# A planned two-layer graph network: attention products of two head groups together, bias reliefs in a way of their own, and some transposes on TensorE

## The chip, the cores and the metric

The kernel runs on one core of one Trainium2 chip. The metric is the device time of one execution in microseconds (us). The time before is the median of three runs, 3202.94 us (3202.18 to 3202.97). All computation is in float32.

## The reference

There are 64 graphs with 256 nodes of 256 features, and an adjacency matrix of zeros and ones for each. Two layers follow each other.

```python
# layer 0
h = _gat(x, adj, W1, a1, Fout)          # Wh = h @ W; e = leaky_relu(Wh @ a[:F] + (Wh @ a[F:]).T)
h = _gat(h, adj, W2, a2, W2.shape[1])   # softmax over axis 1 of where(adj > 0, e, NEG), then @ Wh
h = _layernorm(residual + h, g_ln1, b_ln1)
ff = jnp.matmul(jax.nn.relu(jnp.matmul(h, w_ff1) + b_ff1), w_ff2) + b_ff2
x = _layernorm(h + ff, g_ln2, b_ln2)
# layer 1: q, k, v of 8 heads with 32 features each
scores = jnp.einsum('bhid,bhjd->bhij', q, k) / np.sqrt(dh)
attn = jax.nn.softmax(scores, axis=-1)
for r in range(4):                      # adj holds 0 and 1 only, so two of the four count
    mask = (adj_matrix == r)[:, None]
    out = out + jnp.einsum('bhij,bhjd->bhid', attn * mask, v_r)
x = _ln(src + out @ Wo + bo, g1, beta1)
x = _ln(x + jax.nn.gelu(x @ W1 + b1, approximate=False) @ W2 + b2, g2, beta2)
```

The feed-forward width is 1024.

## The kernel before, in words

The unit of work is a pair of graphs: 32 pairs, each with 512 nodes. `whole_way` (L687) takes one pair from its input to its output: `gat_layers` (L363), `feed_forward` with relu, `attention` (L524), `feed_forward` with gelu (L472), and the store of the result. These functions are generators. Every `yield` ends a step of TensorE work and says which events the next step waits for, the name of a stage that one pair at a time may hold ("gat", "attention" or "ff"), and how many of the eight PSUM banks it takes.

`run` (L208) is a planner that runs while the program is built. It keeps a clock for each engine (`START` sets where they begin) and up to three pairs in progress. At each turn it picks the piece of work that can begin first. On TensorE a step that isn't feed-forward goes ahead of a feed-forward step, so feed-forward fills the gaps of the others. Work for VectorE, ScalarE, GpSimd and the DMA queue of SyncE (SP) is handed in with `put` (L153): an assumed duration, events that it waits for, a rank, and buffers that it needs or frees. `keep_order` (L197) fixes the order found as the order on each engine. Assumed durations thus set the order only; on the chip the engines wait for each other by semaphores.

Stages and lines that matter here:

- **Start.** Constants and weights are loaded on the SP queue in the order in which they are written (L648 to L662). Pair 0's inputs come first, through `load` (L264); for other pairs `load` is put to the plan when the pair before them starts. The loads are xT (input with features on partitions, one buffer), adjT (four buffers) and x (five buffers).
- **Graph layers.** L383 multiplies the input by the weights, `addends` (L288) turns node scores into rows on all partitions, on TensorE for pair 0 (L316) and through DRAM for all others (`row`, `rows`), `gat_weights` (L341) makes the weights e, and L397 and L408 apply them. The stage "gat" is held to the end of the second layer.
- **Layernorm and transposing.** `layernorm` (L421) works on VectorE with a power on GpSimd. `transposed` (L447) turns 32x32 blocks on VectorE (L454), stores them to DRAM (L459, `home`) and gathers them in four DMAs (L465) into yT, the operand with features on partitions. This is done for both graphs of the pair, b = 0 and 1, and at three stages: before the first feed-forward (stage 0 in the change's numbering), before attention (1) and before the second feed-forward (2).
- **Feed-forward.** L483 is 128x512 with eight steps of four matmul records, L499 is 128x256 with eight steps of eight; ScalarE evacuates the first (L486), VectorE adds the second to the rows (L419).
- **Attention.** L520 makes queries and keys, L512 values. The heads of a graph come in two groups of four, so a pair has four groups n. `scores` (L543) multiplies queries and keys in four row tiles of 32 (L550) and takes four banks; ScalarE exponentiates (L557), VectorE masks (L561, `m`, seven buffers) and adds the two halves (L565, `h`, four buffers). `products` (L572) multiplies weights and values in four column tiles of 32 (L579, L582), then VectorE takes reciprocals (L591) and divides (L592). `into_rows` (L596) is the output projection (L601).
- **Reliefs.** Biases are moved into the layernorm offsets; what that adds elsewhere is subtracted again by `relieve` (L669, matmuls at L675) and `relieve_values` (L680, L683). They are steps of pair 0's own way, L692 to L703.

A group's order in attention is written by hand (L605 to L636); its core is:

```python
for n in range(4):
    yield [*masked[n], *valued[:2 + n // 2 * 2]], None, 1
    divided.append(products(n))
    if n < 2:
        yield [], None, 1
        valued.append(values(v[1], 1, n, yT))
        yield [], None, HQ
        scores(n + 2)
```

One written float32 matmul appears in the trace as two matmul records, each with a weight load; a transpose as one.

Of the kernel before, what the change touches and what calls it, by code (L numbers as in the profile page):

```python
# [10 lines left out]
F32 = mybir.dt.float32  # L11
# [7 lines left out]
P = 128  # L19
# [7 lines left out]
MS = 7  # L27
START = {"tensor": 12.0, "vector": 11.0, "scalar": 12.0, "gpsimd": 0.0, "sync": 33.0}
# [3 lines left out]
def two_layers(ctx: ExitStack, tc: tile.TileContext, t: dict, out: bass.AP, flag: bass.AP):  # L32
# [91 lines left out]
    def bank():  # L124
# [12 lines left out]
    free = {name: [0.0] * n for name, n in (("bank", 8), ("a", 2 * HQ), ("m", MS), ("h", HQ), ("yb", 2), ("yT", 3), ("yTa", 1),  # L137
                                             ("xT", 1), ("adjT", 4), ("x", 5))}
# [69 lines left out]
    def run(ways, together):  # L208


        going, ways = [], iter(ways)
        while True:
# [8 lines left out]
            for n, (way, events, name, banks) in enumerate(going):  # L221
                if alone.get(name) in (None, way) and all(e.time is not None for e in events):
                    at = begins("tensor", max([e.time for e in events], default=0.0), "bank" if banks else None, banks)
                    if at is not None:
                        times.append((at, n))
# [8 lines left out]
            if engine == "tensor":  # L234
# [3 lines left out]
                takes("bank", g[3])  # L238
                step = next(g[0], None)
                if step is None:  # L240
                    going.remove(g)
# [22 lines left out]
    def load(pair, at=None):  # L264
# [7 lines left out]
        def adjT():  # L272
            to["adjT"] = io.tile([P, 4, N], I32, name="adjT", bufs=4)
            nc.sync.dma_start(to["adjT"], t["adjT"][rows].rearrange("b (c p) n -> p (b c) n", p=P))

        def x():
            to["x"] = io.tile([P, 4, D], F32, name="x", bufs=5)
# [4 lines left out]
        for emit in (xT, adjT, x):  # L282
            takes(emit.__name__)
# [4 lines left out]
    def addends(y, there, at, layer, pair):  # L288
# [6 lines left out]
        ratio, rows, at_home = small.tile([P, 4], F32, name="ratio"), None, {}  # L295
# [14 lines left out]
        if pair == 0:  # L310
            yield [there], None, 4
            rows, copied = work.tile([P, 8, 4, 32], F32, name="rows"), []
# [9 lines left out]
            return rows, ratio, copied  # L322
# [9 lines left out]
        def spread():  # L332
            nc.sync.dma_start(rows.rearrange("p q n c -> p (q n c)"),
                              at_home["row"].rearrange("j q c -> (j q c)").partition_broadcast(P))

        rows = work.tile([P, 8, 4, 32], F32, name="rows")
        there = put("vector", 0.2, turn, there, rank=0)
        there = put("sync", 0.4, store, there, rank=0, lag=1.9)
        return rows, ratio, [put("sync", 0.4, spread, there, rank=0, lag=3.8)]

    def gat_weights(y, at, rows, ratio, there, to, empty, b):  # L341

        e = work.tile([P, 2, N], F32, name="e", bufs=2)
        sums, rs = small.tile([P, 2], F32, name="sums"), small.tile([P, 2], F32, name="rs")

        def weigh(j):
            k = 2 * b + j
# [806 lines left out]
```

## Time and profile before

| What | Value |
|---|---|
| median of three runs | 3202.94 us |
| profiled execution: time, span | 3197.83 us, 3195.9 us |
| mean granted TensorE clock | 0.993 |
| TensorE (PE) busy | 3146.7 us, 98% |
| VectorE (DVE) busy | 2174.8 us, 68% |
| ScalarE (ACT) busy | 1065.0 us, 33% |
| GpSimd (POOL) busy | 193.0 us, 6% |
| L499 matmuls, both feed-forwards | 919.9 us |
| L483 matmuls, both feed-forwards | 896.2 us |
| L579 and L582 (products), in the chain that ended last | 7.5% and 1.7% of the span |

The span runs from the first to the last instruction on the chip; the execution's own time lies 1.9 us above it. The span is not the median: the three timed runs are executions of their own. Busy times of TensorE overlap, because matmuls are pipelined, so the distance from one start to the next says more than the length of one record. The reader should look at which engine the chain that ended last runs on, at the places where that engine stands idle and for whom it waits, and at how the starts follow each other where it does not stand idle.

### The profile page before, as it was taken

The numbers are of one execution on the slowest core, as the hardware profiler recorded it, in microseconds if no ns is written. First come the engines' busy times: TensorE is split into PE (matmuls) and PEld (weight loads), VectorE is DVE, ScalarE is ACT, GpSimd is POOL, SyncE is SP. The second block draws the span as 40 slices with busy tenths as digits, with TensorE's granted clock in tenths as the row PEclk, the third lists the DMA queues.
The fourth block names the chain that finished last, engine by engine and source line by source line (L and its number), as shares of the span: only waits on it lengthen the run. The fifth ranks groups of instructions, "written<-read, shape, count | busy, mean of one in ns | idle before, by whom it ended". The sixth has DMA issues, their size and how long they took to land.

```text
span 3195.9 us, 44346 instructions
## 1 busy us (share of the span) xinstructions
PE 3146.7 (98%) x16494; PEld 1999.0 (63%) x16494; DVE 2174.8 (68%) x5537; ACT 1065.0 (33%) x1994; POOL 193.0 (6%) x262
## 2 busy tenths in 40 slices
PE   5999999999999999999999999999999999999998
PEld 4666755675576567556756765675567567656645
DVE  3776676767766866767577668667675776686655
ACT  2323323333343233333332432333333324323332
POOL 0000000000000000000000000000000000000000
PEclk8999999999999999999999999999999999999999
DMA  6111311221132123112211321231122113112110
GB/s 199 47 50 63 113 37 57 82 90 34 34 106 67 37 63 113 40 53 83 89 34 34 106 67 37 69 107 43 51 85 87 34 34 113 60 42 65 61 32 28
DMA packets 217438, 211.52 MB, mean 66 GB/s; under 512 B 23040, under 2 KB 175744, under 8 KB 217216
## 3 DMA queue, kind: packets, MB, share of 16 engines
q1 hardware_dynamic: 217216, 208.62, 20.7%
q8 instruction: 132, 2.16, 0.3%
q14 instruction: 90, 0.74, 0.1%
HBM read 141.18 MB, written 67.36 MB: 65 GB/s over the span
## 4 chain that ended last, share of the span: by engine, by line
PE 98%; DMA 1%; SPq 1%; DVE 0%; issue 0%; POOL 0%; POOLq 0%; DVEq 0%
PE ps L499 28%; PE ps L483 28%; PE ps L579 7%; PE ps L512 7%; PE ps L520 7%; PE ps L550 4%; PE ps L601 4%; PE ps L383 3%; PE ps L397 3%; PE ps L408 3%; PE ps L582 2%; DMA ff<-in_L_gnn_bo 0%; DMA xT<-in_xT 0%; SPq L465 0%; DMA yT<-home 0%; PE ps L675 0%
## 5 line engine op out<-in xcount | busy, mean ns | idle before, releaser
L499 PE MATMUL ps<-w_L_gnn_w_ff,ff 128*128 128x256 f32 x2048 | 462.8, 381 | 0.0
L483 PE MATMUL ps<-yT,w_L_gnn_w_ff1p 128*128 128x512 f32 x1024 | 447.4, 594 | 12.1 <-DMA yT<-home 12.1
L499 PE MATMUL ps<-w_L_gnn_W,ff 128*128 128x256 f32 x2048 | 457.1, 381 | 0.0
L483 PE MATMUL ps<-yT,w_L_gnn_W1p 128*128 128x512 f32 x1024 | 448.8, 594 | 7.9 <-DMA yT<-home 7.9
L499 PEld LDWEIGHTS ps<-w_L_gnn_w_ff,ff 128*128 128x128 f32 x2048 | 385.8, 190 | 74.4 <-issue 24.3
L499 PEld LDWEIGHTS ps<-w_L_gnn_W,ff 128*128 128x128 f32 x2048 | 386.7, 190 | 67.3 <-issue 16.5
L561 DVE TENSOR_TENSOR m<-a,adjT 128x512 f32<-128x512 f32 x512 | 339.4, 683 | 76.3 <-ACT a L557 76.3
L557 ACT ACTIVATE a<-ps 128x512 f32<-128x512 f32 x512 | 264.3, 603 | 330.5 <-issue 242.7
L444 POOL TENSOR_TENSOR rstd<-rstd,mhalf 128x2 f32<-128x2 f32 x256 | 192.3, 751 | 2995.9 <-DVE rstd L433 2990.1
L419 DVE TENSOR_TENSOR x<-ps,x 128x512 f32<-128x512 f32 x256 | 173.3, 677 | 263.6 <-PE ps L499 260.6
L483 PEld LDWEIGHTS ps<-yT,w_L_gnn_w_ff1p 128*128 128x128 f32 x1024 | 194.8, 191 | 243.2 <-issue 230.2
L483 PEld LDWEIGHTS ps<-yT,w_L_gnn_W1p 128*128 128x128 f32 x1024 | 194.9, 191 | 235.9 <-issue 219.5
L486 ACT ACTIVATE ff<-ps,c_L_gnn_b_ff 128x512 f32<-128x512 f32 x256 | 175.5, 686 | 445.1 <-PE ps L483 444.7
L514 DVE TENSOR_TENSOR v<-ps,b_L_gnn_bv 128x512 f32<-128x512 f32 x128 | 84.2, 658 | 320.8 <-PE ps L512 320.8
L486 ACT ACTIVATE ff<-ps,c_L_gnn_b 128x512 f32<-128x512 f32 x256 | 175.3, 685 | 345.2 <-PE ps L483 344.9
L512 PE MATMUL ps<-wv,yTa 128*128 128x512 f32 x512 | 247.3, 605 | 0.0
L358 ACT ACTIVATE xw<-xw,rs 128x258 f32<-128x258 f32 (+1 forms) x256 | 116.2, 501 | 375.5 <-DVE rs L353 375.5
L591 DVE RECIPROCAL s<-ps 128x256 f32<-128x256 f32 x128 | 224.1, 1751 | 10.0 <-PE ps L582 10.0
L565 DVE TENSOR_TENSOR h<-a 128x256 f32<-128x256 f32 x512 | 203.6, 418 | 35.3 <-PE ps L582 34.2
L431 DVE BATCH_NORM_STATS2 st<-x 128x6 f32<-128x256 f32 x512 | 207.8, 406 | 2.3
L374 ACT ACTIVATE xw<-ps 128x260 f32<-128x260 f32 (+1 forms) x256 | 97.5, 385 | 326.7 <-PE ps L383 287.3
L348 DVE SCALAR_TENSOR_TENSOR e<-rows,ratio 128x256 f32<-128x256 f32 x256 | 121.9, 476 | 70.7 <-DMA rows<-row 62.7
(96 smaller groups left out, 3412.1 us busy)
## 6 DMA issues: line engine op xcount, KB each, us to landing
home<-yb SPq DMA_DIRECT2D x192, 256.0 KB, 2.1
yT<-home SPq DMA_DIRECT2D x768, 64.0 KB, 2.0
rows<-row SPq DMA_DIRECT2D x62, 512.0 KB, 4.2
xT<-in_xT SPq DMA_DIRECT2D x32, 512.0 KB, 4.5
adjT<-in_adjT SPq DMA_DIRECT2D x32, 512.0 KB, 5.8
x<-in_x SPq DMA_DIRECT2D x32, 512.0 KB, 6.8
out<-x SPq DMA_DIRECT2D x32, 512.0 KB, 3.2
w_L_gnn_w_ff1p<-in_L_gnn_w_ff1p SPq DMA_DIRECT2D x1, 1024.0 KB, 7.9
```

The source lines that it names most:

```text
L431: nc.vector.bn_stats(st[:, j, :], rows[j])
L444: power = put("gpsimd", 0.8, lambda: nc.gpsimd.tensor_tensor(rstd, rstd, mhalf[:, :2], ALU.pow), there)
L483: nc.tensor.matmul(p1, lhsT=w1[:, c, m * P:(m + 1) * P], rhs=yT[c], start=c == 0, stop=c == KC - 1)
L486: there = put("scalar", 0.6, lambda m=m, p1=p1: nc.scalar.activation(f[m], p1, func, bias=b1[:, m:m + 1]), took(1.72), relieved, function= ...
L499: nc.tensor.matmul(p2[:, j * D:(j + 1) * D], lhsT=f[m][:, (2 * j + b) * P:(2 * j + b + 1) * P], rhs=w2[:, m, :], start=m == 0, stop=m == N ...
L512: nc.tensor.matmul(ps, lhsT=yT[:, b, c, jc * P:(jc + 1) * P], rhs=wv[:, c].rearrange("p r m -> p (r m)"), start=c == 0, stop=c == KC - 1)
L520: nc.tensor.matmul(ps, lhsT=w[:, d, c * P:(c + 1) * P], rhs=yT[:, :, d, :], start=d == 0, stop=d == KC - 1)
L557: nc.scalar.activation(a[n][o], ps[o], AF.Exp)
L561: nc.vector.tensor_tensor(m[n][o], a[n][o], adj, ALU.mult)
L565: nc.vector.tensor_tensor(h[n][o], a[n][o][:, :N], a[n][o][:, N:], ALU.add)
L579: nc.tensor.matmul(po[o * DH:(o + 1) * DH, :N], lhsT=v[b][:, jc, at:at + DH], rhs=e[o][:, jc * N:(jc + 1) * N], start=r == jc == 0, stop=r ...
L591: there = put("vector", 1.68, lambda: nc.vector.reciprocal(s, po[:, N:]), there, rank=0)
```

## The change

Five things are changed.

1. In attention, `products` of both head groups of a graph are issued in one step, without another step between them. It waits for the masks of both groups. The two value steps of the second graph follow, then scores 2 and 3, then the products of groups 2 and 3, and then both output projections. The buffers of m and h become eight each.
2. The reliefs leave pair 0's way and become a way of their own, `reliefs`, which runs beside the three pairs until it is done.
3. `hurried` names five stages: stage 0 of pairs 0 and 1, stage 2 of pair 30, stages 1 and 2 of pair 31. There `transposed_on_tensor` replaces the way through DRAM: 16 matmuls by the identity for each graph, in column tiles of 32, into one bank that ScalarE copies out. `addends` uses TensorE for pair 1 as well.
4. Pair 1's inputs are loaded right after the weights of the first feed-forward, ahead of all other weights. adjT has three buffers and x four.
5. The stage "gat" is given up after the first graph layer, and an event keeps the next pair's first application of weights behind the end of the second layer of the pair before. The tiles e and rows are planned as buffers with a due time. Some assumed times differ.

The diff, cut to its core:

```diff
-MS = 7
-START = {"tensor": 12.0, "vector": 11.0, "scalar": 12.0, "gpsimd": 0.0, "sync": 33.0}
+HURRIED = 2
+START = {"tensor": 12.0, "vector": 11.0, "scalar": 12.0, "gpsimd": 0.0, "sync": 40.0}
...
-            for n, (way, events, name, banks) in enumerate(going):
+            for n, (way, events, name, banks, *more) in enumerate(going):
                 if alone.get(name) in (None, way) and all(e.time is not None for e in events):
                     at = begins("tensor", max([e.time for e in events], default=0.0), "bank" if banks else None, banks)
+                    for needs in more:
+                        at = None if at is None else begins("tensor", at, needs)
...
                 step = next(g[0], None)
                 if step is None:
+                    together -= g[0] is besides
...
-        if pair == 0:
-            yield [there], None, 4
-            rows, copied = work.tile([P, 8, 4, 32], F32, name="rows"), []
+        if pair < HURRIED:
+            yield [there], None, 4, "rows"
...
+            yield [e[b][1], *([] if b or not pair else [through_gat[pair - 1]])], None, 2
+            if b == 0:
+                z = work.tile([P, 4, D + 4], F32, name="xw", bufs=2)
...
+        done_with("gat")
+        at_home, ratio, there = yield from addends(z, there, D, 1, pair)
...
+    def hurried(pair, stage):
+
+        return (pair, stage) in ((0, 0), (1, 0), (NPAIR - 2, 2), (NPAIR - 1, 1), (NPAIR - 1, 2))
+
+    def transposed(y, ready, to, b, pair, stage):
+
+        if hurried(pair, stage):
+            to[b] = ready
+            return
...
+    def transposed_on_tensor(y, to):
+
+        for b in range(2):
+            if b == 0:
+                yield [to[b]], None, 1, "yT"
+                to["yT"] = work.tile([P, 2, 4, KC * 64], F32, name="yT", bufs=3)
+            else:
+                yield [to[b]], None, 1
+            p = bank()
+            for c in range(KC):
+                for j in range(2):
+                    for q in range(4):
+                        at = q * 64 + c * 32
+                        nc.tensor.matmul(p[32 * q:32 * q + 32, c * N + j * P:c * N + (j + 1) * P],
+                                         lhsT=y[:, 2 * b + j, at:at + 32], rhs=ident, start=True, stop=True)
+
+            def copy(b=b, p=p):
+                nc.scalar.activation(to["yT"][:, b].rearrange("p a (ck i) -> p ck a i", i=32),
+                                     p.rearrange("p (ck a i) -> p ck a i", a=4, i=32), AF.Copy)
+
+            to[b] = put("scalar", 0.55, copy, took(0.75), frees=["bank"])
+
+    def feed_forward(y, normal, w, func, relieved, gb, pair, stage):
         w1, b1, w2 = w
+        onwards = stage == 0
+        if hurried(pair, stage):
+            yield from transposed_on_tensor(y, normal)
...
-            there = took(2.37)
+            there = took(2.2)
...
-        for n in range(4):
-            yield [*masked[n], *valued[:2 + n // 2 * 2]], None, 1
-            divided.append(products(n))
-            if n < 2:
-                yield [], None, 1
-                valued.append(values(v[1], 1, n, yT))
-                frees_at(clock["tensor"], ["yTa"] * n)
-                yield [], None, HQ
-                scores(n + 2)
-            if n == 2:
-                yield divided[:2], None, 1
-                into_rows(0)
+        for n in (0, 2):
+            yield [*masked[n], *masked[n + 1], *valued[:2 + n]], None, 2
+            divided += [products(n), products(n + 1)]
+            if n == 0:
+                for jc in range(2):
+                    yield [], None, 1
+                    valued.append(values(v[1], 1, jc, yT))
+                frees_at(clock["tensor"], ["yTa"])
+                for later in (2, 3):
+                    yield [], None, HQ
+                    scores(later)
         frees_at(masked[3][-1].time, ["adjT"])
-        yield divided, None, 1
-        into_rows(1)
+        for b in range(2):
+            yield divided[2 * b:2 * b + 2], None, 1
+            into_rows(b)
...
-    landed = {name: at_time(us) for name, us in (("ln0", 14.0), ("ff0", 20.0), ("attention", 31.0), ("ff1", 38.0))}
+    landed = {name: at_time(us) for name, us in (("ln0", 14.0), ("ff0", 23.0), ("attention", 38.0), ("ff1", 45.0))}
     loaded = {0: load(0, 11.0)}
     ln = [layernorm_weights("L0_gnn_g_ln1", "L0_gnn_b_ln1", "L0_gnn_b_ff2")]
     ff0 = (weights("L0_gnn_w_ff1p"), column("L0_gnn_b_ff1"), weights("L0_gnn_w_ff2"))
+    loaded[1] = load(1, 26.0)
...
+    def reliefs():
+        yield [landed["ff0"]], None, 1
+        put("vector", 0.0, lambda: None, relieve(ff0[1], ff0[0], ln[0][2]), event=relieved[0])
+        yield [landed["attention"], *differences], None, 3
+        there = [relieve(bq, wq, ln[1][2]), relieve(bk, wk, ln[1][2]), relieve_values(ln[1][2])]
+        put("vector", 0.15, lambda: nc.vector.tensor_scalar(bqs, bq, SCALE, None, ALU.mult), *there, event=relieved[1])
+        yield [landed["ff1"]], None, 1
+        put("vector", 0.0, lambda: None, relieve(ff1[1], ff1[0], ln[2][2]), event=relieved[2])
...
+    run(reliefs(), (whole_way(pair) for pair in range(NPAIR)), 3)
```

## The prediction

> **What bounds the kernel now.** I read the busy times first, then the chain that ended last, then TensorE's own waits, then its timeline.
>
> ```profile
> PE 3146.7 (98%) x16494; PEld 1999.0 (63%) x16494; DVE 2174.8 (68%) x5537; ACT 1065.0 (33%) x1994; POOL 193.0 (6%) x262
> PE 98%; DMA 1%; SPq 1%; DVE 0%; issue 0%; POOL 0%; POOLq 0%; DVEq 0%
> ```
>
> TensorE (PE) is the bound, and the chain is TensorE nearly throughout. VectorE (DVE) comes second, a third idle. Between 200 and 3050 us the list of TensorE's waits is empty. So only three things can shorten this kernel: less TensorE work, fewer lost moments between matmuls that follow each other, or a smaller idle head and tail. The idle is all here:
>
> ```profile
> 21.49 5.61 PE L397 MATMUL ps<-xw,e 128*128 128x258 f32 x16 [4.06 <-ACT xw L358]
> 31.81 5.41 PE L408 MATMUL ps<-xw,e 128*128 128x256 f32 x16 [2.81 <-ACT xw L358]
> 44.10 6.28 PE L383 MATMUL ps<-w,xT 128*128 128x260 f32 x16 [3.42 <-DMA xT<-in_xT]
> 62.49 3.75 PE L483 MATMUL ps<-yT,w_L_gnn_w_ff1p 128*128 128x512 f32 x4 [12.11 <-DMA yT<-home]
> 102.42 0.95 PE L675 MATMUL ps<-c_L_gnn_boc,w_L_gnn_Wqp 128*128 128x1 f32 x8
> ...
> 3097.49 6.99 PE L483 MATMUL ps<-yT,w_L_gnn_W1p 128*128 128x512 f32 x12 [7.87 <-DMA yT<-home]
> ```
>
> Columns are start, length, instructions, and in brackets the idle time before. The two largest waits are for yT, the transposed rows that go through DRAM. The reliefs after 102 us stand in a stretch that is already full. After each idle time the matmuls are slow: 16 of L397 take 5.61 us here, 3.76 later.
>
> The middle, attention of one pair:
>
> ```profile
> 1075.31 1.88 PE L520 MATMUL ps<-yTa,w_L_gnn_Wkp 128*128 128x512 f32 x4
> 1077.03 1.88 PE L512 MATMUL ps<-wv,yTa 128*128 128x512 f32 x4
> 1078.84 1.15 PE L550 MATMUL ps<-qT,kT 32*128 32x256 f32 x16
> 1079.91 1.98 PE L520 MATMUL ps<-yTa,w_L_gnn_Wqp 128*128 128x512 f32 x4
> 1081.73 1.88 PE L520 MATMUL ps<-yTa,w_L_gnn_Wkp 128*128 128x512 f32 x4
> ...
> 1100.56 1.07 PE L579 MATMUL ps<-a,v 128*32 128x256 f32 x16
> 1101.44 1.05 PE L579 MATMUL ps<-m,v 128*32 128x256 f32 x16
> 1102.31 0.61 PE L582 MATMUL ps<-h,ones 128*32 128x256 f32 x8
> 1102.85 1.99 PE L601 MATMUL ps<-w_L_gnn_Wo,oT 128*128 128x256 f32 x8
> ```
>
> Lengths overlap, so read from start to start. L520 before L512 takes 1.72 us; L512 before the scores (L550) takes 1.81; L520 after the scores takes 1.82. Nothing waits there: about 0.1 us is lost at every change of tile shape.
>
> [...] here 4 L483 after 12.11 us of idle take 3.75 us, later 1.88.
>
> **Part 1, products in one stretch.** Single records of the trace give the price of a shape change. A group of four tiled matmuls repeats every 216 ns, 128x512 every 429.
> - Into a tiled stretch: 522 instead of 429, +0.093 us. First matmul after it: 533 instead of 429, +0.104.
> - Scores: second group 320 (+0.104), leaving 324 (+0.108).
> - Products: second group 240 (+0.024), leaving 329 (+0.113).
>
> So products alone lose 0.093+0.024+0.113+0.104 = 0.334 us, scores alone 0.093+0.104+0.108+0.104 = 0.409, and scores directly followed by products 0.093+0.104+0.108+0.024+0.113+0.104 = 0.546. Over all records I count 53 joined stretches, 75 scores alone and 75 products alone: 28.9+30.7+25.1 = 84.7 us. After: 64 double products lose 21.4, and 128 scores alone 52.4. The double ones need masks of the scores just made (four ACT operations of 0.6 and eight DVE operations, 4 x (0.68+0.42) = 4.4 us), so they hardly follow scores at once and the joined stretches go. Sum 73.7: **gain 11.0**. In the new order scores 2 and 3 can touch if eight banks are free; the two products and two values before them hold four, feed-forward one more, so I assume one pair in four: 8 x 0.409 = **3.3** (0 to 13.1).
>
> The price is a longer wait inside attention: about 5.5 us from second scores to products, some 8 after the fourth, 4.5 for two reciprocals (1.75 each) and divisions before the second output projection, together some 18 us instead of 11. Feed-forward of other pairs, 4 x 13.8 = 55 us per pair, covers it; uncovered it is TensorE idle. Behind a waiting product on TensorE queue all other pairs' matmuls. In the trace the last mask or half is ready 0.7 to 3.3 us ahead of its product. The plan prices mask and half at 0.61 and 0.36 (0.68 and 0.42 measured), so eight run 0.5 us late. With steps of 1.72 us I let a quarter of 64 stretches wait 0.25 us: **loss 4** (0 to 25).
>
> **Part 2, head: reliefs in idle time, pair 1 early, transposes for pairs 0 and 1.** Idle before: 7.34+0.52+0.90+4.06+0.81+2.81+3.42+12.11 = 32.0. The first four (12.8) precede other available work and stay. After that the first relief (3.6 us, already in idle time), pair 1's first products (3.8) and later products, and the attention reliefs (4, now in the full part) can fill. Pair 0's rows are normalised at 42 and 44; from there its feed-forward needs two transposes and copies, about 46 instead of 62.5. I leave 3.7 us of new idle: 16.5, so 15.5 gained (10 to 19). Slow-clock excess is 1.85 (L397)+1.79 (L408)+2.61 (L383)+1.87 (L483) = 8.1; the first and about 1.7 stay, 4.5 gained.
>
> Added: each transposed half is 16 multiplications, two records each as at L579, so 8 groups of four. Width is half of L579's: 0.108 us if it scales, 0.216 if a floor holds. I take 0.13 (L316, 128 columns: 1.06/8), the weight load being 0.11: 1.04+0.334 = 1.37 us (1.2 to 2.1). Four halves: 5.5. Pair 1's row transposes: 2 x 1.06 = 2.1. **Head: 15.5+4.5-5.5-2.1 = gain 12.4** (4 to 18).
>
> Queues: on SP pair 1's three loads (0.4 to 0.6 us each) pass all attention weights. The xT issue waits for L383 to have read the old xT (15.4 us); SP stood at 15.5 there, so that wait costs under 1 us, and the 1.5 MB behind it some 5 us at about 350 GB/s. Attention weights come 5 us later, needed at 102 in before: covered. Each hurried stage takes two stores, eight gathers (0.43 each) from SP and two 0.70 turns from DVE, and gives ACT two copies of some 0.6: ACT is 33% busy, nothing. POOL keeps its work. Fewer x and adjT buffers cost nothing, as loads land in 5.8 to 6.8 us and a pair has 97; the early release of the graph stage gives nothing where TensorE is full.
>
> **Part 3, tail.** The idle 7.87 and the slow 1.7 after it go: pair 30's second projection starts at 3080.8, its rows can be ready near 3088, and work lasts until 3089.3. Added six halves, 8.2; next is pair 31's second output, with less filler: 1. **Gain 9.6-8.2-1 = 0.4** (-4 to 4). The last 10 us (normalise, store) stay.
>
> **Sum.** 11.0+3.3-4+12.4+0.4 = 23.1. The profiled execution took 3197.83 (span 3195.9 and 1.9 around it): 3174.7. The median of runs is 5.1 above it, 3202.94: **3180**.
>
> **Rivals.**
> - Larger: scores 2 and 3 touch in every pair (+9.8) and no products wait (+4): 3166. For it: banks empty quickly when feed-forward is in its second half. Against: that half holds a bank. 12%.
> - Head gives nothing, because late weights or transposes of 2.1 us (+7.3 over ten) eat it: 3192 to 3195. For it: the DMA engines are at 0.8 to 0.9 in the first 50 us. Against: pair 1's loads pass the attention weights, and only pair 0's own inputs and the first feed-forward's weights stay ahead. 10%.
> - Within 0.2%: waits of some 0.4 us per stretch cancel all: 3200. 8%.
> - Slower: the double products' wait becomes TensorE's bound. 23.1+4 over 64 stretches: from 0.42 us each the gain is gone, and from 0.53 us it is over 6.4 us (0.2%) slower. At 0.7 us: 3180-4+45 = 3221. For it: each stretch waits for twice the masks, and the plan underprices DVE by a tenth. Against: no wait of any kind on TensorE in 2850 us now. 10%.
> - That products are not adjacent: excluded, both are emitted in one step and the order is fixed.
>
> The forecast has 60%, 3170 to 3190. The range reaches to the larger gain and to the lost head: 3164 to 3196. Faster by over 0.2% (about what a measurement of this kernel can tell from no change): 82%, same 8, slower 10.
>
> **What would show it.** 80 tiled records of L579 and L582 in a row in about 4.5 us, 64 such stretches; no TensorE wait in the middle (right) or an entry at L579 from DVE (wrong); first feed-forward near 46 us; reliefs before 60 us; a tiled 128-column group at 0.13 us; no 7.87 gap at 3089. A loss of more than 0.4 us at each double stretch would make the prediction wrong.

## The result, and the profile after

| | median | range | runs |
|---|---|---|---|
| after | 3214.3 us | 3211.77 to 3217.1 | 6 |
| before, on the same chip | 3202.56 us | 3197.13 to 3203.07 | 6 |

The changed kernel takes 1.0041 of the time before (95% interval 1.0028 to 1.0054). It is slower by 12 us, where 23 us less were predicted. The profiled execution took 3215.46 us with a span of 3213.5 us and a mean granted clock of 0.996.

Busy times and the chain that ended last, from the page of after:

```profile
PE 3157.0 (98%) x16830; PEld 2016.3 (63%) x16830; DVE 2182.1 (68%) x5525; ACT 1085.4 (34%) x2030; POOL 193.9 (6%) x262
...
PE 75%; DVE 15%; DMA 8%; issue 1%; ACT 1%; SPq 0%; POOL 0%; DVEq 0%; POOLq 0%; ACTq 0%
```

TensorE is as busy as before, but the chain has changed: only 75% of it lies on TensorE now, where it was 98%. That does not mean that TensorE stands idle for a quarter of the span: the chain goes over to VectorE and DMA wherever TensorE had to wait at all, and follows them back from there. How long TensorE waits between 200 and 3060 us, and where, its list of waits says (for whom, us in total, times, longest; idle times under 0.15 us are not listed). In the kernel before, this list is empty:

```profile
PE ps L409 <- ACT xw L368: 28.8, 27, 2.8
```

L409 applies the weights of the first graph layer (L397 before). It waits 27 times, about once in each pair. How the 17.6 us between the two spans came about is read from a sum that I call **lost time**: elapsed time less each matmul record at the distance at which its kind repeats without a stop (0.429 us at 512 columns, 0.216 at 256, 0.219 and 0.2175 at 260 and 258, 0.054 in a group of four tiles; transposes, reliefs and the start at nothing). The ideal is 3034.0 us for both kernels. It is cut by the work done, counted in ideal time: the first 200 us, up to 2900, the rest.

| lost time, us | head | middle | tail | after the last matmul |
|---|---|---|---|---|
| before | 63.1 | 74.2 | 15.1 | 9.4 |
| after | 47.8 | 103.9 | 18.4 | 9.2 |
| predicted change | -12.4 | -10.3 | -0.4 | 0 |
| measured change | -15.3 | +29.7 | +3.4 | -0.2 |

The head is better than predicted. The middle is where the prediction fails, by 40 us, so first to what could have been slow there and isn't. The double products, TensorE's timeline of one pair in after (start, length, instructions):

```profile
1083.52 1.07 PE L629 MATMUL ps<-a,v 128*32 128x256 f32 x16
1084.41 1.05 PE L629 MATMUL ps<-m,v 128*32 128x256 f32 x16
1085.27 0.61 PE L632 MATMUL ps<-h,ones 128*32 128x256 f32 x8
1085.70 1.05 PE L629 MATMUL ps<-a,v 128*32 128x256 f32 x16
1086.57 1.05 PE L629 MATMUL ps<-m,v 128*32 128x256 f32 x16
1087.43 0.61 PE L632 MATMUL ps<-h,ones 128*32 128x256 f32 x8
1087.97 3.70 PE L560 MATMUL ps<-wv,yTa 128*128 128x512 f32 x8
```

80 records in 4.45 us from start to start, and no bracket behind any L629: no product waits for its masks.

Now a pair whose L409 waits, from the timeline of all engines in after; the issues of DMAs stand under SPq:

```profile
952.19 13.90 PE L531 MATMUL ps<-yT,w_L_gnn_w_ff1p 128*128 128x512 f32 x32
...
952.97 0.39 SPq L755 DMA_DIRECT2D out<-x  x1
...
954.25 0.24 DVE L333 STREAM_TRANSPOSE blocks<-rise 128x64 f32<-128x64 f32 x1
...
954.52 0.54 SPq L337 DMA_DIRECT2D row<-blocks  x1
...
957.63 0.37 SPq L284 DMA_DIRECT2D x<-in_x  x1
...
959.06 0.34 SPq L341 DMA_DIRECT2D rows<-row  x1
...
964.61 0.48 DVE L358 SCALAR_TENSOR_TENSOR e<-rows,ratio 128x256 f32<-128x256 f32 x1 [5.16 <-DMA rows<-row]
...
967.71 0.91 ACT L368 ACTIVATE xw<-xw,rs 128x258 f32<-128x258 f32 x2 [4.33 <-DVE rs L363]
...
968.27 4.13 PE L409 MATMUL ps<-xw,e 128*128 128x258 f32 x10 [2.18 <-ACT xw L368]
```

And the same piece of a pair in the timeline of before:

```profile
923.49 0.54 SPq L330 DMA_DIRECT2D row<-blocks  x1
...
926.30 0.34 SPq L333 DMA_DIRECT2D rows<-row  x1
...
930.52 0.48 DVE L348 SCALAR_TENSOR_TENSOR e<-rows,ratio 128x256 f32<-128x256 f32 x1 [2.14 <-DMA rows<-row]
...
934.81 3.64 PE L397 MATMUL ps<-xw,e 128*128 128x258 f32 x16
```

Read it as a race. The node scores leave TensorE with L393, are turned on VectorE (L333), stored as a row (L337), spread over all partitions (L341), made into weights (L358) and into scaled rows on ScalarE (L368); then L409 may start. In its place TensorE runs eight steps of feed-forward, 13.7 us, and that number is the planner's: it stands in both kernels. In before the rows are used 4.2 us after their issue (926.30 to 930.52) and TensorE never stops. In after it is 5.55 us (959.06 to 964.61), and 2.18 us are lost. Beside the rows two transfers of 512 KB are at work: the store of a finished pair (out), and the load of the next x, which had to wait for that store, because x has four buffers instead of five. SyncE's own waits in after, 200 to 3090 us:

```profile
SPq L284 <- DMA out<-x: 37.5, 13, 4.4
```

There is no such line in before. Mean over pairs 2 to 31, worked out from the starts in the traces, for all kernels that matter (us; a "gap" of 0.43 from the start of the last record before L409 to L409 is no wait):

| kernel | turn to row store | to spread | to first weight | turn to first weight | first weight to L409 | gap |
|---|---|---|---|---|---|---|
| before | 0.28 | 2.84 | 4.32 | 7.44 | 4.32 | 0.43 |
| after | 0.29 | 3.31 | 5.52 | 9.13 | 3.74 | 1.54 |
| x late | 0.29 | 3.12 | 4.85 | 8.26 | 3.87 | 0.83 |
| weights in one piece | 0.39 | 3.55 | 5.11 | 9.06 | 3.05 | 0.55 |
| "gat" to the end | 0.36 | 3.68 | 4.91 | 8.95 | 4.03 | 0.78 |
| plan told 5.6 us | 0.37 | 2.92 | 6.02 | 9.31 | 5.16 | 0.35 |
| small x load | 0.28 | 3.21 | 4.99 | 8.48 | 3.83 | 0.98 |
| small x load and out store | 0.28 | 2.44 | 4.54 | 7.26 | 4.60 | 0.52 |

The plan itself believes 6.85 us from turn to first weight (0.2 for the turn, 0.15 for handing it on, 0.4 and 1.9 for the store, 0.4 and 3.8 for the spread). Before took 0.6 us more than that, and after takes 2.3 more. The gaps of after add up to 46.2 us over these 30 pairs, those of before to 12.9: 33.3 us are lost there. Another 2.8 us go at the second record of L409, and 3.1 to a lower clock: behind its two longest waits, of 2.18 and 2.79 us, TensorE runs at half the clock for 3.41 us each. One of the two (window; length; busy time of PE, PEld, DVE, ACT, POOL; granted clock; DMA share; GB/s):

```profile
968.90:972.20 3.30, 3.30 (x9) 2.55 (x8) 0.00 (x0) 2.32 (x6) 0.00 (x0) 0.50 0.16 43
```

These make 39 us. The middle loses 29.7 more than before, so some 9 are gained in it elsewhere, most of them by the double products (experiment 2).

Where the path grew can be read from the landing times of the same transfers. From turn to first weight it is 1.69 us longer than in before. The row store lands 0.19 us later (2.92 us after its issue, 2.73 in before), the spread is issued 0.28 later after that landing (0.39, 0.11 in before), and the spread itself lands 1.20 later (5.35, 4.15 in before). So most of it is transfers that take longer, and a smaller part is the spread's wait for its turn on the queue. In the 27 pairs of after in which the load or the store was under way for over 0.5 us beside the spread, it lands after 5.51 us, in the other three after 3.99.

### The profile page after: what moved, and what is told of

Read it like the earlier page. It is cut to its first block, busy times and chain, and to the rows that moved or that the text cites. A ratio compares the mean times of both kernels' runs of the same rounds, so it can differ in the third digit from the quotient of the medians.

```text
span 3213.5 us, 44988 instructions
## 1 busy us (share of the span) xinstructions
PE 3157.0 (98%) x16830; PEld 2016.3 (63%) x16830; DVE 2182.1 (68%) x5525; ACT 1085.4 (34%) x2030; POOL 193.9 (6%) x262
## 4 chain that ended last, share of the span: by engine, by line
PE 75%; DVE 15%; DMA 8%; issue 1%; ACT 1%; SPq 0%; POOL 0%; DVEq 0%; POOLq 0%; ACTq 0%
PE ps L547 24%; PE ps L531 16%; PE ps L568 7%; PE ps L560 7%; PE ps L629 7%; DMA rows<-row 5%; PE ps L600 4%; PE ps L409 4%; PE ps L651 3%; DVE e L360 2%; DVE e L358 2%; DVE st L447 2%; DVE x L435 2%; DMA out<-x 2%; PE ps L632 2%; DVE x L453 2%
## 5 line engine op out<-in xcount | busy, mean ns | idle before, releaser
L611 DVE TENSOR_TENSOR m<-a,adjT 128x512 f32<-128x512 f32 x512 | 350.9, 685 | 112.9 <-ACT a L607 112.9
L368 ACT ACTIVATE xw<-xw,rs 128x258 f32<-128x258 f32 (+1 forms) x256 | 115.9, 500 | 418.9 <-DVE rs L363 418.9
L560 PE MATMUL ps<-wv,yTa 128*128 128x512 f32 x512 | 238.7, 599 | 0.0
L615 DVE TENSOR_TENSOR h<-a 128x256 f32<-128x256 f32 x512 | 214.1, 418 | 0.0
L358 DVE SCALAR_TENSOR_TENSOR e<-rows,ratio 128x256 f32<-128x256 f32 x256 | 122.2, 477 | 126.5 <-DMA rows<-row 116.8
```

Source lines behind the costliest of these rows:

```text
L560: nc.tensor.matmul(ps, lhsT=yT[:, b, c, jc * P:(jc + 1) * P], rhs=wv[:, c].rearrange("p r m -> p (r m)"), start=c == 0, stop=c == KC - 1)
L611: nc.vector.tensor_tensor(m[n][o], a[n][o], adj, ALU.mult)
L615: nc.vector.tensor_tensor(h[n][o], a[n][o][:, :N], a[n][o][:, N:], ALU.add)
```

## The experiments

Each median stands beside that of the kernel before in the same batch; the bracket is the 95% interval of the ratio. Before moves by up to 1.7 us between these batches, so a difference between kernels of two batches holds to a microsecond or two.

**1. One cause at a time.** The fewer buffers alone on the kernel before; the double products with their buffers on it; x's load put behind its own pair's rows; and the plan told the longer landing of the rows.

```diff
 # b_buf, on before
-                                             ("xT", 1), ("adjT", 4), ("x", 5))}
+                                             ("xT", 1), ("adjT", 3), ("x", 4))}
 # b_pp, on before: as b_buf, m and h eight each, and the products' and output projections' order of the change
 # a_xlate, on after: the x load is put to the plan only when the pair's own rows are under way
+        if "load x" in to:
+            put("sync", 0.5, to["load x"], *there, rank=3, lag=4.0, needs="x", event=loads[2])
 # a_rowlag, on after
-        return at_home, ratio, [put("sync", 0.4, spread, there, rank=0, lag=3.8, needs="rows")]
+        return at_home, ratio, [put("sync", 0.4, spread, there, rank=0, lag=5.6, needs="rows")]
```

> The kernel before with one edit: x in four buffers and adjT in three, as in the change. Theory (the load of x now waits for the output store, stands on the SP queue between the row store and the spread of rows, and shares the DMA engines with it, so the graph layer's weights come late and TensorE waits at its first application): this alone makes TensorE wait at L397 in most pairs, 0.5 to 1.5 us each, 3215 to 3240 us. Rival (early release of the graph stage or the merged products cause the waits): no waits at L397, 3203 within 3 us.

> The kernel before with the products of both head groups in one stretch and the buffers that this needs (m and h eight each, x four, adjT three), nothing else of the change. My prediction had a gain of 9 to 11 us from the fewer changes of tile shape. Theory: that gain is there, but the graph layer's first application waits as in the changed kernel, 20 to 35 us, so about 3215 to 3225. Rival (the waits come from the early release of the graph stage): no waits, about 3192.

> The changed kernel, with the load of x planned only once the pair's own rows of the first graph layer are spread, so that it no longer stands between row store and rows. x is needed only at the end of the second graph layer. Theory: most of the 33 us of waits at the first application of the graph weights go, 3182 to 3192. Rival (the rows are late by themselves, or the stage's early release puts the step too early): the waits stay, 3208 to 3216.

> The changed kernel, with one number of the plan altered: the spread of rows is assumed to land 5.6 us after its issue in place of 3.8 (the trace of the changed kernel shows 5.3 to 6.2 from issue to the first use). Nothing on the chip becomes faster; the plan only places the graph step later and other TensorE work before it. Theory: TensorE has other work at that point, so the waits mostly go, 3182 to 3195. Rival (no other TensorE work is there at that time): unchanged at 3214.

Measured, against 3199.41: b_buf 3207.45, 1.0024 [1.0016, 1.0033]; b_pp 3206.02, 1.002 [1.0013, 1.0028]; a_xlate 3190.49, 0.9968 [0.9956, 0.998]; a_rowlag 3177.9, 0.993 [0.9917, 0.9944].

One number of the plan takes the changed kernel from 1.0041 to 0.993 of before, some 35 us. The rows are not used sooner for it: they land after 4.82 us (5.35 in after) but are used after 6.02. What it does is that the planner puts other work in front of the weights and of L409. What is left of the waits from 200 to 3060 us in a_rowlag:

```profile
PE ps L409 <- ACT xw L368: 1.4, 1, 1.4
PE ps L568 <- ACT yTa L583: 0.4, 1, 0.4
```

So enough other work was there: in 28 of the 30 pairs 15.5 or 17.2 us of steps now stand ahead of L409, and the middle loses 66.0 us instead of 103.9. Fewer buffers cost 8 us in before too, though L397 waits only 3.0 us there: its lost time grows in the middle (74.2 to 82.5) and a little in the head (63.1 to 65.1). The rows come later there too (4.93 instead of 4.32 us). The list of waits shows only a part: by the starts of its records, L397 loses 8.6 us in the middle of b_buf (0.3 in before), 4.4 at its first record and the rest at its second and at the first two of the second graph, much of it in stops too short for the list. Both b_buf and b_pp were expected to take 3215 us or more; waits of the size of those in after did not come. The double products on top of it give 9.6 us in the middle (82.5 to 72.9) and lose 11.3 in the tail (14.7 to 26.0), where without transposes TensorE waits 16.5 us for the last pair's attention operand.

**2. Other ways to shorten the race; the parts of the gain.** On after: both weights of a graph as one piece, and "gat" held to the end of the second layer as before. On a_rowlag: products apart as before (r_nopp), no transposes in the last pairs (r_notail).

```diff
 # a_weigh, on after
-        there = put("vector", 0.9, lambda: weigh(0), *there, rank=0, needs="e")
-        there = put("vector", 1.0, lambda: weigh(1), there, rank=0, frees=["rows"] * b)
+        there = put("vector", 1.9, lambda: (weigh(0), weigh(1)), *there, rank=0, needs="e", frees=["rows"] * b)
 # a_nogat, on after: done_with("gat") stands at the end of the second layer
 # r_notail, on a_rowlag
-        return (pair, stage) in ((0, 0), (1, 0), (NPAIR - 2, 2), (NPAIR - 1, 1), (NPAIR - 1, 2))
+        return (pair, stage) in ((0, 0), (1, 0))
```

> The changed kernel, with both weight computations of a graph planned as one piece of VectorE work, as they in effect were before. In the changed kernel the two are chained, the plan slips the other graph's first one between them, and TensorE's first application starts no earlier than 3.66 us after the first weight operation, against 2.74 in the kernel before with fewer buffers. Theory (the plan knows this order and is only mistaken about when the rows land): the plan moves the step forward as well, the waits stay, 3208 to 3216. Rival (the interleaving itself costs the waits, 29 times 0.92 us): 3187 to 3193.

> The changed kernel, with the graph stage held to the end of its second layer, as before. Theory (rows land later than planned, beside the load of x and the output store): the waits stay, 3206 to 3218. Rival (the early release lets the next pair's transfers and steps come too close): the waits go, 3182 to 3192.

> The version with the corrected landing time of the rows (3177.9 us), with the products of the two head groups apart again, in the order and with the buffers m and h of the kernel before. By the price of the shape changes (joined scores and products 53 times, 75 of each alone, against 64 double stretches and 125 stretches of scores) the single products should cost 9 to 11 us more: 3186 to 3190. Rival (the double products' longer wait gives the gain back elsewhere): 3174 to 3180.

> The version with the corrected landing time of the rows (3177.9 us), with the last two pairs' transposes through DRAM again and those of the first two still on TensorE. My prediction had 0.4 us of gain from the tail, which is nothing: 3178. Rival (with double products the last pairs have too little other work, so the way through DRAM stands open, as the 16.5 us wait at the queries of the last pair in the kernel with the double products alone suggests): 3182 to 3190.

Measured, against 3198.66: a_weigh 3198.48, 0.9995 [0.9989, 1.0002]; a_nogat 3195.08, 0.9987 [0.998, 0.9993]; r_nopp 3181.19, 0.9945 [0.9931, 0.9958]; r_notail 3184.47, 0.9956 [0.9942, 0.9969].

a_weigh and a_nogat each take most of the waits away (3.6 and 11.4 us are left from 200 to 3060 us), as the late load of x does (9.1). In a_weigh and a_nogat they had been expected to stay. The three do it in different ways, and the late load is the cleanest test of them. The late load leaves the 13.7 us of feed-forward as they are in 27 of 30 pairs, and makes the path from turn to first weight 0.87 us shorter (9.13 to 8.26). The one piece is worth 0.7 us from first weight to L409 (3.74 to 3.05): with two chained pieces the planner slips a weight of the other graph between them; but in 9 pairs the planner has also put 1.7 us more ahead of L409. With "gat" held to the end the path is hardly shorter (8.95), and 19 pairs have some 15.5 us ahead of L409. So the gains can't be added: once the path fits under the work ahead, more of either gives nothing. (a_weigh loses 14 us in its head, for a reason told under 6.)

r_nopp, between its two expectations, says what the double products are worth when nothing waits: 3.3 us. In the middle they save 8.1 (74.1 to 66.0), in the tail they cost 6.6 (12.3 to 18.9), where too little work is left between two stretches. r_notail says, as its rival had it, that the last transposes are worth 6.6 us beside double products. Without them, TensorE in the tail:

```profile
PE ps L568 <- ACT yTa L583: 17.0, 2, 16.5
```

**3. Parts of the head, and a plan for before.** On a_rowlag: no transposes for pairs 0 and 1 (r_nohead); reliefs back in pair 0's way (r_norelief); one-piece weights and late x together (r_weigh_x). On b_buf: its weights chained as in the change (b_chain), which was expected to wait.

```diff
 # r_nohead
-        return (pair, stage) in ((0, 0), (1, 0), (NPAIR - 2, 2), (NPAIR - 1, 1), (NPAIR - 1, 2))
+        return (pair, stage) in ((NPAIR - 2, 2), (NPAIR - 1, 1), (NPAIR - 1, 2))
 # b_chain, on b_buf
-        weighed = [put("vector", 0.9 + 0.1 * j, lambda j=j: weigh(j), *there, rank=0) for j in range(2)]
-        return e, put("scalar", 0.85, scale, *weighed, rank=0)
+        there = put("vector", 0.9, lambda: weigh(0), *there, rank=0)
+        there = put("vector", 1.0, lambda: weigh(1), there, rank=0)
+        return e, put("scalar", 0.85, scale, there, rank=0)
```

> The version with the corrected landing time of the rows (3177.9 us), with the transposes of the first two pairs through DRAM again; the last pairs' stay on TensorE, reliefs and the early load of pair 1 stay. My prediction let pair 0's feed-forward begin 16 us earlier by these transposes, so it counted most of 12 us to them: 3186 to 3191. Rival (pair 1's early inputs and the reliefs fill the head anyway): 3176 to 3181.

> The version with the corrected landing time of the rows (3177.9 us), with the bias reliefs at their old places in pair 0's own way. My prediction counts 7 us of reliefs that move from a full stretch into idle time: 3182 to 3186. Rival (the idle time of the head is filled by other work, so nothing is gained by the reliefs): 3176 to 3180.

> The version with the corrected landing time of the rows (3177.9 us), with both weights of a graph in one piece and the load of x behind the rows, to shorten the chain itself. Theory: the waits there are gone already (1.4 us left), so at most 2 us more: 3174 to 3180. Rival (a shorter chain lets the graph layers run ahead and frees TensorE elsewhere): below 3172.

> The kernel before with x in four and adjT in three buffers (3207.5 us alone) and, in addition, the two weight computations of a graph chained in the plan as in the changed kernel, which puts the other graph's first one between them. Theory (rows that land late and weights that take 0.92 us more until the first application add up against 13.7 us of feed-forward steps; neither is enough alone): waits at the first application grow from about 4 us to 10 to 20 us in all, 3211 to 3222. Rival (the plan sees the chain and moves the step by a whole feed-forward step): 3204 to 3209.

Measured, against 3198.46: r_nohead 3174.56, 0.9927 [0.9914, 0.9941]; r_norelief 3180.49, 0.9944 [0.993, 0.9957]; r_weigh_x 3188.79, 0.9969 [0.9957, 0.9981]; b_chain 3208.89, 1.0035 [1.0022, 1.0049].

r_nohead has the lowest time of all, 24 us below before: the transposes for the first two pairs cost 2 to 3 us (3.3 between the medians of two batches) and buy nothing, where they had been expected to give 8 or more. The reliefs are worth 2.6 us, less than expected. r_weigh_x and b_chain are misses; the first is told under 6. The weights of b_chain are longer under way (4.88 us from first weight to L397), but the planner saw that and put one step more ahead of L397 in all but one of pairs 2 to 31: it starts 15.7 us or more after the last input product, where that is mostly 13.95 in b_buf. No wait grew (3.0 us left). So the chained weights alone make no wait where the plan counts them.

**4. The same order on every engine, less traffic.** In the experiments above the planner may reorder. a_xsmall and a_xout leave every engine's order as in after. From pair 4 on, a_xsmall loads one of four blocks of x, and adds the bias row of the values in place of the residual; a_xout also stores only one of four blocks of the result.

```diff
 # a_xsmall, on after
+            some = 4 if pair < 4 else 1
-            nc.sync.dma_start(to["x"], t["x"][rows].rearrange("b (c p) d -> p (b c) d", p=P))
+            nc.sync.dma_start(to["x"][:, :some], t["x"][rows].rearrange("b (c p) d -> p (b c) d", p=P)[:, :some])
 # a_xout, on a_xsmall
-            out[2 * pair:2 * pair + 2].rearrange("b (c p) d -> p (b c) d", p=P), to["x"]),
+            out[2 * pair:2 * pair + 2].rearrange("b (c p) d -> p (b c) d", p=P)[:, :some], to["x"][:, :some]),
```

> The changed kernel with every engine's order exactly kept, in which the load of x brings only one of its four blocks (128 KB in place of 512) from pair 4 on; the residual of the first layernorm is then left out there and a bias row is added in its place, at the same cost. Only the traffic beside the rows is less. Theory (rows share the DMA engines with x): spread to first weight falls from 5.5 us to about 4.8, waits at the first application from 33 us to about 15, 3192 to 3202. Rival (the rows are late for reasons of order alone): 3210 to 3217.

> As the one before, and the output store also writes only one of its four blocks from pair 4 on, so that the x load behind it is released earlier too; three quarters of the output are then left out. Theory (x and the store before it explain the late rows): spread to first weight near 4.4 us and row store to spread near 2.9, as in the kernel before, waits below 8 us, 3183 to 3192. Rival (the shorter weights chain or the order is what matters): 3200 or more.

Measured, against 3197.74: a_xsmall 3197.44, 0.9998 [0.999, 1.0007]; a_xout 3176.2, 0.9929 [0.9916, 0.9943].

The waits from 200 to 3060 us, of a_xsmall and then of a_xout:

```profile
PE ps L410 <- ACT xw L369: 12.7, 16, 1.7
```

```profile
PE ps L410 <- ACT xw L369: 2.3, 4, 0.7
```

This shows the cause. With the order of all engines held, taking bytes away from the load and the store brings the waits from 28.8 over 12.7 to 2.3 us, the rows' use from 5.52 over 4.99 to 4.54 us after their issue, and the middle's loss from 103.9 over 83.3 to 67.4. a_xout is even below its expected range. It shortens the load's wait on SyncE's queue as well (22.8 us in 13, from 37.5), and the way from store to spread (3.31 to 2.44); but of the 1.87 us that the path gains, 0.64 are an earlier landing of the row store (2.28 us after its issue), 0.23 an earlier issue of the spread behind it, and 0.96 an earlier landing of the spread (4.39). Whether a transfer lands late because it shares the DMA engines or because its packets stand behind the load's is not told apart.

**5. The plan's number turned the other way, and the early load undone.** On before, the landing of the rows planned too early by 3.3 us more; on r_nohead, pair 1's inputs loaded as in before.

```diff
 # b_lag05, on before
-        return rows, ratio, [put("sync", 0.4, spread, there, rank=0, lag=3.8)]
+        return rows, ratio, [put("sync", 0.4, spread, there, rank=0, lag=0.5)]
 # r_noearly, on r_nohead
-        frees_at(clock["tensor"], ["xT"] * (pair > 0))
+        frees_at(clock["tensor"], ["xT"])
...
-    loaded[1] = load(1, 26.0)
```

> The kernel before with one number of the plan altered the other way: the spread of rows is assumed to land 0.5 us after its issue in place of 3.8. The plan then puts seven in place of eight feed-forward steps between the input products and the first application of the graph weights, 12.0 us against a chain of about 12.5. Theory (a plan that thinks the rows early makes TensorE wait, whatever else is in the change): waits at L397 of 5 to 20 us, 3203 to 3218. Rival (the chain has room): 3196 to 3201.

> The version with the corrected landing time and the first pairs' transposes through DRAM (3174.6 us), with pair 1's inputs no longer loaded ahead of the attention weights. The head of the changed kernel loses 15 us less than before, and neither the transposes (3.3 us faster without them) nor the reliefs (2.6 us) account for it. Theory (pair 1's early products fill the head): 3184 to 3192. Rival (the order of the weights does not matter, the reliefs' way and the graph stage's early release do it): 3173 to 3178.

Measured, against 3197.74: b_lag05 3360.18, 1.0501 [1.0487, 1.0516]; r_noearly 3184.75, 0.9958 [0.9944, 0.9971].

The direction is as expected: the kernel before, with nothing else changed, gets the new wait. Its waits from 200 to 3060 us:

```profile
PE ps L397 <- ACT xw L358: 50.7, 18, 3.7
PE ps L408 <- ACT xw L358: 35.5, 27, 3.1
```

The number acts on the rows of both graph layers, so L408 waits too. The size is badly missed: 162 us, of which these waits are 86. The middle loses 221.7 us, 147.5 more than before. By the starts of the records, 94.7 of them are waits (the middle's work lasts beyond 3060 us here), 30.8 are matmuls at half the clock, and 22 are lost at the first matmuls behind a wait and in stops too short for the list. The granted clock falls to half 14 times between 200 and 3060 us, for 3.41 or 6.83 us, each time within 5 us of the start of a wait of 2.4 to 3.7 us. One of them:

```profile
1331.11 6.75 PE L397 MATMUL ps<-xw,e 128*128 128x258 f32 x16 [3.68 <-ACT xw L358]
```

```profile
1330.40:1337.20 6.80, 6.09 (x14) 4.88 (x15) 2.05 (x8) 4.02 (x9) 0.00 (x0) 0.50 0.01 2
```

r_noearly loses 10.2 us to r_nohead, in the head (55.0 to 45.7 lost). Pair 0's feed-forward starts at 70.5 us instead of 64.65. So the early load is what shortens the head most.

**6. Why two kernels with fewer waits have a bad head.** r_weigh_x hardly waits in the middle (64.5 lost), but loses 62.6 in its head, 14 more than a_rowlag. A window of its profile, in the columns used above, then the same one of a_rowlag:

```profile
47.00:70.00 23.00, 22.16 (x99) 18.25 (x100) 8.65 (x30) 3.46 (x8) 0.69 (x1) 0.50 0.01 2
```

```profile
47.00:70.00 23.00, 23.00 (x167) 17.48 (x166) 15.16 (x52) 11.95 (x31) 0.94 (x1) 1.00 0.26 79
```

And TensorE's timeline of r_weigh_x at that place:

```profile
47.84 3.81 PE L411 MATMUL ps<-xw,e 128*128 128x258 f32 x8 [3.52 <-ACT xw L369]
...
58.27 6.83 PE L728 MATMUL ps<-c_L_gnn_b2c,w_L_gnn_W1p 128*128 128x1 f32 x32
```

After a wait of 3.52 us the clock stays at half for 23 us, though TensorE is busy for 22.16 of them; the same 32 reliefs take 3.63 us in after. a_weigh shows the same waits and lengths (3.53 and 6.83 us). The stretch holds 10.4 us of one-column reliefs and 1.93 us of transposes by the identity, with short runs of full matmuls (3.72 to 3.81 us each) between. That the reliefs and the transposes kept the clock at half is my guess. One sign is for it: in after the clock falls to half at 50.66 us, for 3.41 us, 12 us after the last listed wait and 1 us behind a stretch of 7 us of reliefs, and L409 takes 5.41 us. One is against: in a_rowlag the same 7 us of reliefs are followed by no fall, and L409 takes 3.73. No run measured it by itself.

## Why the prediction was wrong, point by point

- **Fewer buffers: the step that failed.** "Fewer x and adjT buffers cost nothing, as loads land in 5.8 to 6.8 us and a pair has 97; the early release of the graph stage gives nothing where TensorE is full." The load is in time, as said. But where it runs was not asked: it starts when the store of the old pair ends, and both fall beside the rows of the pair after, whose path has 13.7 us. b_buf measured +8 us for the buffers alone; in after, the traffic's part is 36.5 us of the middle's loss (103.9 to 67.4, a_xout). And the plan's numbers were taken for an order only, when the other work that they put ahead of L409 is what a delay must stay within. The second half of the sentence fails with the first: with "gat" held (a_nogat) 17 us of the waits are gone. The times for which load and store are under way during a spread add up to 4.0 us on average in after, to 2.1 in b_buf and 1.7 in a_nogat, so the early release seems to move them onto the rows; a_nogat also has more work ahead of L409, and no run has the early release with five buffers for x, so the parts of the two are not told apart.
- **Chained weights** were not priced at all: with one piece the path from first weight to L409 is 0.7 us shorter (a_weigh).
- **Shape changes: right.** Lost at tiled stretches in the attention, from the record before each stretch to the second one behind it: 84.6 us before (84.7 by the prices of the prediction), 73.3 after (without a wait of 1.13 us), 11.3 gained where 11.0 were predicted. A double stretch of 80 records takes 4.45 us. Touching scores came once only, in the tail (3140.44 us), so that term (3.3) was nothing. In the middle the double products give 8.1 (r_nopp).
- **Waits at products: predicted 4, measured 0.** The rival "slower" had the right kind, a wait that takes TensorE in every pair, at the wrong place.
- **Head: 12.4 predicted, 15.3 measured, for another reason.** The early load gives 10.2 (r_noearly), the reliefs 2.6 (r_norelief), the transposes -3.3 (r_nohead), 9.5 in all. The other 6 have no test of their own; a_nogat, where the stage is not given up early, loses 6 us more in its head than after, so they may be the early release. That the number came near is luck: the transposes, which were to start the feed-forward early, cost time. Feed-forward of pair 0 began at 61.62 us, not at 46: pair 1's L409 (49.62, 5.41 us long) and further products of the input stand ahead of it. Reliefs were all done by 50 us, as predicted.
- **A transposed half: 1.21 us, predicted 1.37** (1.2 to 2.1), with what is lost at its entry and behind it, where it stands between full matmuls (3165.64 us): the groups of four repeat every 0.109 us, the scaled value.
- **Tail: +0.4 predicted, -3.4 measured.** The wait moved instead of going away. In after:

```profile
3103.75 1.08 PE L508 MATMUL ps<-ident,x 128*32 128x128 f32 x32
3109.37 4.29 PE L508 MATMUL ps<-ident,x 128*32 128x128 f32 x96 [4.54 <-DVE x L457]
3114.16 1.98 PE L568 MATMUL ps<-yTa,w_L_gnn_Wqp 128*128 128x512 f32 x4 [0.50 <-ACT yTa L583]
...
3143.58 8.85 PE L531 MATMUL ps<-yT,w_L_gnn_W1p 128*128 128x512 f32 x20 [1.13 <-ACT a L607]
```

  The 7.87 us for yT are gone, but 4.54 us pass before the last pair's rows are normalised, and little feed-forward is left to fill them. The prediction let the double products cost nothing here; by r_nopp they cost 6.6.

The sum without the failed step would have stood: with the waits removed by one number (a_rowlag) the changed kernel is 21.5 us faster than before, where 23.1 were predicted. That is luck in part, for its terms are others: some 15 us of the head, 8 of the middle and a loss of 4 in the tail, where 12.4, 10.3 and 0.4 were predicted.

## What to carry to other kernels

When a change touches buffers or transfers, don't ask only whether the load is in time: ask what it now runs beside, which transfers on a TensorE path stand in its queue or are under way at the same time (load and store beside a spread for 4.0 us on average in after), and how many microseconds of other work cover that path. Where a planner writes the order, compare each assumed landing time with the measured one before believing that "no wait" will last: before stood 0.6 us off its plan without a sign, and in after, 2.3 us off, 33 us are lost at L409. A repair may then be a better number rather than less work.

## What was not expected of the hardware

- With a load and a store of 512 KB each near in time, the broadcast of rows (it writes 512 KB too) is used 1.2 us later on average (5.52 us after its issue, 4.32 in before); with a quarter of their bytes it is 4.54. From the list of the tile rows in after:

```profile
DMA to landing us min/median/max: 3.3/4.5/6.3
```

  Before has a median of 4.2 and a longest of 4.7: the longest transfers grow most.
- The granted clock stayed at half for 23 us on a TensorE that was 96% busy (experiment 6).
- Waits of 2.18 and 2.79 us (after) and of 2.4 to 3.7 us (b_lag05) were followed by half the clock for 3.41 or 6.83 us, so a wait can cost more than its length. A landing planned 3.3 us earlier, with nothing else changed, made the kernel 5% slower (b_lag05), and 31 of the 162 us are this.
